# Bias seeds from ScalarE in a graph-network kernel: four layer-1 chunks of ten get their bias written into PSUM, and TensorE adds to it

## The chip, the cores and the metric

The kernel runs on one core of one Trainium2 chip. The metric is device time in microseconds (us), the median of three runs. The core has five engines with queues of their own: TensorE (PE in the profile, its weight loads PEld), VectorE (DVE), ScalarE (ACT), GpSimd (POOL) and SyncE (SP), whose queue issues most DMAs. Matmul results land in PSUM, eight banks of 512 float32 per partition. One instruction waits for another through semaphores, counters that an engine raises when an instruction ends.

## The reference

A message-passing layer over 128 graphs of 64 nodes with 128 channels. For each edge (i, j) a three-layer perceptron runs on the pair of node features; messages are masked by the adjacency matrix and summed over j; a second perceptron updates the node, with a residual.

```python
def _mlp(x, w0, b0, g0, be0, w1, b1, g1, be1, w2, b2):
    h = jax.nn.relu(x @ w0 + b0)
    h = _layernorm(h, g0, be0)
    h = jax.nn.relu(h @ w1 + b1)
    h = _layernorm(h, g1, be1)
    return h @ w2 + b2
pair_feats = jnp.concatenate([f_i, f_j], axis=-1)
messages = _mlp(pair_feats, msg_w0, ...) * coupling_matrix[..., None]
agg = jnp.sum(messages, axis=2)
upd_in = jnp.concatenate([part_feats, agg], axis=-1)
return part_feats + _mlp(upd_in, upd_w0, ...)
```

About one adjacency entry in seven is set, and the kernel computes only those.

## The kernel before

Edges are compacted: each of 64 pairs of graphs gets 2 x 640 slots, and slots are worked in chunks of 512 (four tiles of 128 edges). There are 160 chunks; five chunks are one quad of graphs `q`, ten one block `b` of eight graphs. The program is unrolled, and its order is written by hand: iteration `n` of the last loop runs layer 0 of chunk `n`, the statistics of chunk `n - 1`, and layer 1 of chunk `n - 8` (`L1 = 8`). Around these, `at(n, place, fn)` puts other work at fixed places of an iteration: "a" and "m" before layer 1, "b" between layer 1 and layer 0, "x" after the statistics, and so on. Each engine runs its own instructions strictly in the order in which the loop writes them. Two places matter most:

- **Layer 1** (`layer1`). The layer norms are folded: the layer-1 result of an edge is `relu(h @ w1c + std0 * b1b)`, where `std0` is the edge's standard deviation after layer 0, and `b1b` a bias row spread over 128 partitions. Before the change TensorE makes the term `std0 * b1b` itself. The root `m_sd` (ScalarE, `root0`) is split in a high and a low half `sh` (ScalarE, then GpSimd, L541 and L542), transposed by TensorE (L547, `turn_root`), copied to `sdT` (ScalarE, L552), and used as the weights of one 80x512 matmul against the table `b1t` (L561) that opens the PSUM bank `z`. Four pairs of `w1c` matmuls (L564) add the layer. ScalarE then writes `y` = relu(`z`) (L567). There is one `z` bank, so the next chunk's first matmul waits until `y` has read it; there is one `hps` bank for layer 0, emptied by ScalarE's `h` (L517).
- **The update unit** (`Unit`). Once a block, some twenty iterations later, a chain of steps runs for 512 nodes: `ysum`, transposes, a layer `uh`, its statistics, its root `um_sd`, `upd_shift` (ScalarE: four 128x128 copies `usdb` = `bu1b` times a column of `um_sd`, L724), a layer `uy` that adds `usdb`, and the output. `STEADY` lists the iterations of these steps for the first thirteen blocks.

In the steady part the work of an iteration depends on the last digit of its number. Iterations 4, 9 and 2 carry little besides the two layers; 8 and 3 carry 40 short matmuls of the message sums `ys` and 16 of the next rows `mu`; 5, 6, 7, 0 and 1 carry steps of the update. At iterations 1 and 6 the quad's root `m_sd` is taken. ScalarE also makes, per pair of graphs, `d` (L460) and the 32-bit copy `i` (L472), and per block `abh`, `xnT` and small copies.

The program's functions that the change touches:

Of the kernel before, what the change touches and what calls it, by code (L numbers as in the profile page):

```python
# [13 lines left out]
AF = mybir.ActivationFunctionType  # L14
# [9 lines left out]
def tile_gnn(  # L24
# [40 lines left out]
    nc = tc.nc  # L65
# [7 lines left out]
    QT = 4 * TG  # L73
    CH = 4
    QC = QT // CH
    NCHK = NQ * QC
    PB = 4
    NB = NP // PB
    CPB = NCHK // NB
# [88 lines left out]
    W = {}  # L168
# [83 lines left out]
    def root0(stp, m2, n, name):  # L252

        sd = stp.tile([P, n], F32, name=name + "_sd")
        nc.scalar.activation(sd, m2, AF.Sqrt, scale=1.0 / C, bias=eps_c)
        return sd
# [28 lines left out]
    def edge_path(es):  # L285
# [9 lines left out]
        stp = es.enter_context(tc.tile_pool(name="stp", bufs=5))  # L295
# [19 lines left out]
        def zbank():  # L315
            return ps_z.tile([P, CH, C], F32, name="z").rearrange("p t c -> p (t c)")
# [4 lines left out]
        def at(n, place, fn, *args):  # L321
            plan.setdefault((n, place), []).append((fn, args))
# [3 lines left out]
                fn(*args)  # L326

        blocks = {b: {} for b in range(NB)}
        TP, S, H, ST0, V0, SD, SH, Y, ST1, Q, OH, WT, YS, MK, D, IR, JR = ({} for _ in range(17))


        def load_adj(b):
# [196 lines left out]
        def eng_of(q):  # L529

            return nc.vector if q == NQ - 1 else nc.gpsimd
# [3 lines left out]

        def root_of(q):

            sd = root0(stp, V0[q], QT, "m20")
            SH[q] = lp.tile([P, 4, QT], F32R, name="sh", bufs=2)
            sdb = sd.unsqueeze(1).to_broadcast([P, 2, QT])  # L540
            nc.scalar.copy(SH[q][:, 0:2, :], sdb)  # L541
            eng_of(q).tensor_tensor(SH[q][:, 2:4, :], sdb, SH[q][:, 0:2, :].bitcast(F32),  # L542
                                    op=ALU.subtract)
# [6 lines left out]
        def root_out(q):  # L550
            t = lp.tile([4 * QT, P], F32R, name="sdT")
            nc.scalar.copy(t, SD[q][0:4 * QT, 0:P])  # L552
            SD[q] = t

        def layer1(n):

            q, c = divmod(n, QC)
            ps = (hbank if n >= NCHK - L1 and n % 2 else zbank)()
            ps = ps.rearrange("p (t c) -> p t c", t=CH)
            h = H.pop(n)  # L560
            nc.tensor.matmul(ps, lhsT=SD[q], rhs=W["b1t"][:, CH * c:CH * c + CH, :], start=True,  # L561
                             stop=False, skip_group_check=True)
            for t in range(CH):
                nc.tensor.matmul(ps[:, t, :], lhsT=h[:, t * P:(t + 1) * P], rhs=W["w1c"],  # L564
                                 start=False, stop=True, skip_group_check=True)
            Y[n] = yp.tile([P, CH, C], F32, name="y")
            nc.scalar.activation(Y[n], ps, AF.Relu)  # L567
# [92 lines left out]
        def wide(name, u):  # L660

            if name not in u.blk:
                u.blk[name] = updp.tile([P, PB, C], F32, name=name,
                                        bufs=2 if name in ("uo", "xo", "m0") else 1)
            return u.blk[name][:, u.q, :]
# [29 lines left out]
        def layer(u, *pairs):  # L695
            ps = u.bank()
            for q in range(u.n):
                s = slice(q * P, (q + 1) * P)
                for n, (src, w) in enumerate(pairs):
                    l = (u.blk["xnT"][:, (u.k0 + q) * P:(u.k0 + q + 1) * P] if src == "xn" else  # L700
                         getattr(u, src)[:, s])
                    nc.tensor.matmul(ps[:, s], lhsT=l, rhs=w, start=(n == 0),
                                     stop=(n == len(pairs) - 1))
            u.l_ps = ps[:, 0:u.n * P].rearrange("p (q c) -> p q c", q=u.n)
# [13 lines left out]
        def upd_root0(u):  # L718
            u.sd = root0(updp, u.m2, u.n, "um0" + u.tag)

        def upd_shift(u):
            u.usdb = wide("usdb", u)
            for q in range(u.n):
                nc.scalar.activation(u.usdb[:, q, :], W["bu1b"], AF.Copy, scale=u.sd[:, q:q + 1])  # L724

        def upd_m1(u):
# [21 lines left out]
        L1 = QC + 3  # L748
        SC = QC + L1 + QC

        STEADY = (1, 2, 3, 3, 4, 7, 8, 6, 8, 9, 12, 13, 11, 14, 15)
# [26 lines left out]
        for b in reversed(range(NB)):  # L778
            o = b * CPB
            n = o + QC + SC  # L780

            if b < NB - 1:
                t = STEADY if b < NB - 3 else LAST[b - NB + 3]
                units = [(Unit(b, 0, PB, nc.gpsimd, ubank), n, t, 0, t[5] - 1)]
                if b == NB - 2:
                    units = [units[0][:3] + (-5, -4)]
            else:
                units = [(Unit(b, 2, 2, nc.vector, zbank), NCHK + L1 + 1, LAST[3], 1, 1),
                         (Unit(b, 0, 2, nc.gpsimd, hbank), NCHK + L1 - 1, LAST[2], 3, 3)]
            for u, n, t, m0_at, xo_at in units:  # L790
                at(n + m0_at, "m", bias0, u)
                at(n + xo_at, "e", residual, u)
                at(n + t[0], "a", sums_out, u)
                at(n + t[1], "x", turn, u, "ysum")
                at(n + t[2], "a", turn_out, u, "ysum")
                at(n + t[3], "x", lambda u: layer(u, ("xn", u0a), ("ysumT", W["w2u"])), u)
                at(n + t[4], "m", layer_out, u, "uh", "m0")
                at(n + t[4], "e", upd_m0, u)
                at(n + t[5], "x", turn, u, "uh")
                at(n + t[6], "a", turn_out, u, "uh")  # L800
                at(n + t[7], "a", upd_root0, u)
                at(n + t[7], "x", upd_shift, u)
                at(n + t[8], "x", lambda u: layer(u, ("uhT", W["u1c"])), u)
                at(n + t[9], "m", layer_out, u, "uy", "usdb")
                at(n + t[9], "e", upd_m1, u)
                at(n + t[10], "x", turn, u, "uy")
                at(n + t[11], "a", turn_out, u, "uy")
                at(n + t[12], "a", upd_root1, u)
                at(n + t[12], "m", upd_inverse, u)
                at(n + t[13], "x", lambda u: layer(u, ("uyT", W["u2c"])), u)  # L810
                at(n + t[14], "m", finish, u)
        for p in range(NP):
            n = p * TG * 2 // CH
            if p > 1:
                at(max(n - 7, p - 2), "a", distance, p)
                at(max(n - 6, p - 2), "m", make_tp, p)
                at(max(n - 5, 1), "a", node_rows, p)
                at(max(n - 4, 1), "a", stack, p, 0, IR)
                for k in range(2):
                    at(n - 5 + k, "k", marks, p, k)  # L820
                    at(n - 5 + k, "k", compare, p, k)
                at(n - 3, "a", stack, p, 1, JR)
            w = p // 2 * QC + QC + L1 + p % 2
            last = p // 2 == NQ - 1
            at(w - 4, "a", node_marks, p)
            q, h = divmod(p, 2)
            for g in range(2):
                wait = h + 2 if q == NQ - 3 else h + 1 if q == NQ - 2 else 2 + (2 * h + g + 1) // 2
                at(*((NCHK + L1, "b") if last else (q * QC + QC + L1 + wait, "e1")), weights, p, g)
            at(NCHK + L1 + 1 if last else q * QC + SC - (q >= NQ - 3), "x1", reduce, p)  # L830
        for q in range(NQ):
            n = q * QC + QC
            last = q == NQ - 1
            at(n, "e0", var0_of, q)
            at(*((n, "e1") if last else (n + 1, "b")), root_of, q)
            at(*((n + 2, "b") if last else (n + 1, "x")), turn_root, q)
            at(n + 2, "x" if last else "a", root_out, q)
            at(n + L1 - last, "e1", var1_step, q)
            wait = 0 if last else 1 if q == NQ - 2 else 2
            at(n + L1 + wait, "a", root1_of, q)  # L840
            at(n + L1 + wait, "m", inverse_of, q)
# [26 lines left out]
        for g in range(2):  # L868
            s = slice(g * N, (g + 1) * N)
            nc.scalar.copy(S[0][0:N, g, :], TP[0][s])  # L870
            for k in range(2):
                c = slice(k * HC, (k + 1) * HC)
# [68 lines left out]
        for n in range(last + 1):  # L941
            run(n, "a")
            run(n, "m")
            if n == NCHK:
                stats0(n - 1)
            if 0 <= n - L1 < NCHK:
                layer1(n - L1)
            run(n, "b")
            if n < NCHK:
                layer0(n)  # L950
            if 0 <= n - 1 < NCHK - 1:
                stats0(n - 1)
            run(n, "k")
            if 0 <= n - L1 < NCHK:
                stats1(n - L1)
            for k in ("x", "x1", "x2", "e0", "e1", "e"):
                run(n, k)
# [3 lines left out]
    with ExitStack() as es:  # L961
        es.enter_context(tc.manual_schedule())
        flag = edge_path(es)
# [160 lines left out]
```

## Time and profile before

| what | value |
|---|---|
| median of three runs | 613.35 us (612.3 to 613.7) |
| profiled execution | 612.8 us, its span 611.1 us |
| TensorE busy | 574.7 us, 94% of the span |
| VectorE busy | 479.3 us, 78% |
| ScalarE busy | 397.2 us, 65% |
| GpSimd busy | 294.8 us, 48% |
| the `b1t` matmul, L561 into `z` | 156 times, mean 492 ns |
| layer-1 output `y`, L567 from `z` | 156 times, mean 597 ns |
| update copy `usdb`, L724 | 64 times, mean 396 ns |

The span is the stretch that the profiler sees; the time of the execution has 1.7 us more around it. In a row of the timeline the first number is the start in us from the start of the span, the second the length of the row in us, then engine, line, operation and `out<-in`; `x4` means four instructions merged into a row; square brackets give how long the engine was idle before the row and what released it. A mean length contains latency: instructions of one engine overlap at their ends, and what counts for the queue is the distance of starts.

### The profile page before, as it was taken

Reading aid. Unit: us, or ns where it says so; the run is one execution under the profiler, and the core shown is the slowest. Engines: PE = TensorE matmul, PEld = TensorE weight load, DVE = VectorE, ACT = ScalarE, POOL = GpSimd, SP = SyncE. Lnnn points to the kernel's source line nnn. Section 1 sums busy time; section 2 is a strip of 40 time slices with the busy share of each in tenths; the row PEclk is TensorE's granted clock in tenths of the full one; section 3 lists DMA queues with packets and bytes.
Section 4 is the critical chain, followed back from the end, with each engine's and each line's share of the span. In section 5 each row is a group of like instructions: output and inputs, shape, how many; then the busy total and the mean of one; then the engine's idle time right before and its main releaser. Section 6 shows DMA issues by size and latency. Waiting matters only on the chain. (4 is left out here: it accounts for less than half of the span.)

```text
span 611.1 us, 15571 instructions
## 1 busy us (share of the span) xinstructions
PE 574.7 (94%) x5393; PEld 530.1 (87%) x5393; DVE 479.3 (78%) x1947; ACT 397.2 (65%) x845; POOL 294.8 (48%) x837
## 2 busy tenths in 40 slices
PE   5798999999999999999999999999999999999895
PEld 4687889898989989898998989899898989989884
DVE  5767687886969788696978869697886969787675
ACT  5675666776666577666657766665776666566334
POOL 1632355644626564462656446265644626545352
PEclk7899999999999999999999999999999999999998
DMA  4554445455455655545453454545344354431201
GB/s 115 141 126 117 106 110 130 80 124 99 102 137 105 132 85 123 99 102 140 107 129 84 123 101 102 139 108 131 79 124 101 93 140 99 108 85 33 62 18 39
DMA packets 91087, 63.86 MB, mean 105 GB/s; under 512 B 57462, under 2 KB 74876, under 8 KB 91004
## 3 DMA queue, kind: packets, MB, share of 16 engines
q1 hardware_dynamic: 90716, 62.69, 44.7%
q8 instruction: 44, 0.72, 0.5%
q14 instruction: 39, 0.32, 0.2%
q10 hardware_dynamic: 288, 0.13, 0.1%
HBM read 6.82 MB, written 4.19 MB: 18 GB/s over the span
## 5 line engine op out<-in xcount | busy, mean ns | idle before, releaser
L527 DVE BATCH_NORM_STATS2 st<-hT 128x6 f32<-128x128 f32 x640 | 141.3, 283 | 63.0 <-PE hT L523 62.9
L564 PEld LDWEIGHTS z<-w1c,h 128*128 128x128 f32 x1248 | 164.1, 192 | 6.8
L564 PE MATMUL z<-w1c,h 128*128 128x128 f32 x1248 | 164.6, 275 | 0.0
L567 ACT ACTIVATE y<-z 128x512 f32<-128x512 f32 x156 | 93.1, 597 | 71.8 <-PE z L564 71.2
L574 DVE BATCH_NORM_STATS2 st<-y 128x6 f32<-128x128 f32 x640 | 137.6, 277 | 2.7 <-ACT y L567 1.4
L245 POOL TENSOR_TENSOR m_d<-st 128x20 f32<-128x20 f32 x62 | 17.1, 276 | 229.7 <-DVE st L527 206.3
L517 ACT ACTIVATE h<-hps,b0c 128x512 f32<-128x512 f32 x160 | 109.5, 684 | 2.5 <-PE hps L514 2.4
L523 PE MATMUL hT<-ident,h 128*128 128x128 f32 x640 | 97.2, 275 | 1.1 <-DVE st L527 1.1
L630 POOL TENSOR_TENSOR w<-oh,m_q 128x320 f32<-128x320 f16 x126 | 91.4, 742 | 10.1 <-PE hT L523 5.5
L514 PE MATMUL hps<-s,abl 128*128 128x512 f32 (+3 forms) x256 | 92.3, 373 | 0.4 <-ACT h L517 0.4
L561 PE MATMUL z<-b1t,sdT 80*128 80x512 f32 x156 | 76.7, 492 | 11.7 <-ACT y L567 11.7
L523 PEld LDWEIGHTS hT<-ident,h 128*128 128x128 f32 x640 | 76.3, 141 | 11.1 <-ACT h L517 1.3
L514 PE MATMUL hps<-s,abh 128*128 128x512 f32 (+3 forms) x256 | 78.5, 325 | 0.0
L444 ACT CAST abh<-mu 128x512 fp32r<-128x512 f32 x32 | 18.8, 586 | 91.1 <-PE mu L437 91.1
L643 PE MATMUL ys<-y,w 128*64 128x128 f32 x1280 | 76.9, 275 | 0.0
L643 PEld LDWEIGHTS ys<-y,w 128*64 128x64 f32 x1280 | 69.2, 137 | 7.0 <-issue 6.6
L496 DVE TENSOR_TENSOR j<-mk,cmpt 128x320 fp32r<-128x320 f32 x126 | 59.7, 474 | 1.6 <-PE mk L488 1.6
L460 ACT ACTIVATE d<-slot,mid 128x640 f16<-128x640 f16 x64 | 53.4, 834 | 0.0
L514 PEld LDWEIGHTS hps<-s,abl 128*128 128x128 f32 x256 | 49.5, 193 | 1.8 <-ACT i L472 0.9
L514 PEld LDWEIGHTS hps<-s,abh 128*128 128x128 f32 x256 | 49.6, 194 | 0.0
L561 PEld LDWEIGHTS z<-b1t,sdT 80*128 80x128 f32 x156 | 29.4, 189 | 21.9 <-ACT y L567 15.1
L472 ACT CAST i<-tp 128x640 fp32r<-128x640 f16 x63 | 45.3, 719 | 1.9 <-DVE tp L466 1.9
(215 smaller groups left out, 972.5 us busy)
## 6 DMA issues: line engine op xcount, KB each, us to landing
s<-i SPq DMA_DIRECT2D x126, 160.0 KB, 2.7
s<-j SPq DMA_DIRECT2D x126, 160.0 KB, 2.6
xn<-in_x_dram SPq DMA_DIRECT2D x15, 256.0 KB, 3.9
out_dram<-uo SPq DMA_DIRECT2D x15, 256.0 KB, 2.4
an<-in_adj_dram SPq DMA_DIRECT2D x16, 128.0 KB, 2.6
oh<-tp SPq DMA_TRANSPOSE x64, 2.7
xn<-in_x_dram SPq DMA_DIRECT2D x2, 128.0 KB
out_dram<-uo SPq DMA_DIRECT2D x2, 128.0 KB
```

Source lines behind the costliest of these rows:

```text
L460: nc.scalar.activation(D[p], slot, AF.Abs, bias=blocks[b]["mid"][:, q:q + 1], scale=-1.0)
L496: nc.vector.tensor_tensor(JR[p][:, c], MK.pop((p, k))[:, 0:HC], cmpt[:, c], op=ALU.is_equal)
L514: nc.tensor.matmul(ps[:, c:c + w], lhsT=ab[:, g % 4, :], rhs=s, start=(k == 0), stop=(k == 1))
L517: nc.scalar.activation(H[n], ps, AF.Relu, bias=b0c)
L523: nc.tensor.transpose(ps[:, t, :], H[n][:, t * P:(t + 1) * P], ident)
L527: nc.vector.bn_stats(ST0[q][:, CH * c + t, :], ps[:, t, :])
L561: nc.tensor.matmul(ps, lhsT=SD[q], rhs=W["b1t"][:, CH * c:CH * c + CH, :], start=True, stop=False, skip_group_check=True)
L564: nc.tensor.matmul(ps[:, t, :], lhsT=h[:, t * P:(t + 1) * P], rhs=W["w1c"], start=False, stop=True, skip_group_check=True)
L567: nc.scalar.activation(Y[n], ps, AF.Relu)
L574: nc.vector.bn_stats(ST1[q][:, CH * c + t, :], Y[n][:, t, :])
L630: (nc.vector if p == NP - 2 else nc.gpsimd).tensor_tensor(WT[p][:, :, g, :], OH[p][:, :, g * N:(g + 1) * N], Q[q][:, k:k + TG].unsqueeze(2 ...
L643: nc.tensor.matmul(YS[b][g * N:(g + 1) * N, k, :], lhsT=w[:, t, g, :], rhs=y, start=(t == 0), stop=(t == TG - 1))
```

## The change

For each chunk `n` from 1 to 150 whose last digit is 0, 1, 6 or 9, sixty chunks in all, ScalarE writes `std0 * b1b` into the `z` bank with four 128x128 activations ("seeds"), straight from the root `m_sd` and `b1b`. They are put at "b" of iteration `n + 7`, so behind the `y` that empties the bank and ahead of that iteration's `h`; by last digit they stand in iterations 7, 8, 3 and 6. In iteration 6 they stand ahead of the root `m_sd` too, which the plan puts behind them at the same place. One iteration later these chunks have no `b1t` matmul: the first `w1c` matmul adds to what is in the bank. The transposes and `sdT` stay, since the other chunks use them. Second, in blocks on the `STEADY` list the four `usdb` copies are no longer issued together: one in iteration 9, one in 0, two in 1.

```diff
+        def seed(n):
+            q, c = divmod(n, QC)
+            Z[n] = zbank().rearrange("p (t c) -> p t c", t=CH)
+            for t in range(CH):
+                k = CH * c + t
+                nc.scalar.activation(Z[n][:, t, :], W["b1b"], AF.Copy, scale=SR[q][:, k:k + 1])
...
         def layer1(n):
-            ps = (hbank if n >= NCHK - L1 and n % 2 else zbank)()
-            ps = ps.rearrange("p (t c) -> p t c", t=CH)
             h = H.pop(n)
-            nc.tensor.matmul(ps, lhsT=SD[q], rhs=W["b1t"][:, CH * c:CH * c + CH, :], start=True,
-                             stop=False, skip_group_check=True)
+            if n in Z:
+                ps = Z.pop(n)
+            else:
+                ps = (hbank if n >= NCHK - L1 and n % 2 else zbank)()
+                ps = ps.rearrange("p (t c) -> p t c", t=CH)
+                nc.tensor.matmul(ps, lhsT=SD[q], rhs=W["b1t"][:, CH * c:CH * c + CH, :],
+                                 start=True, stop=False, skip_group_check=True)
...
-        def upd_shift(u):
-            u.usdb = wide("usdb", u)
-            for q in range(u.n):
+        def upd_shift(u, q0, q1):
+            if q0 == 0:
+                u.usdb = wide("usdb", u)
+            for q in range(q0, q1):
                 nc.scalar.activation(u.usdb[:, q, :], W["bu1b"], AF.Copy, scale=u.sd[:, q:q + 1])
...
-                at(n + t[7], "x", upd_shift, u)
+                if t is STEADY:
+                    for k, q0, q1 in ((0, 0, 1), (1, 1, 2), (2, 2, PB)):
+                        at(n + t[7] + k, "x", upd_shift, u, q0, q1)
+                else:
+                    at(n + t[7], "x", upd_shift, u, 0, u.n)
...
+        for n in range(1, NCHK - L1 - 1):
+            if n % CPB in (0, 1, 6, 9):
+                at(n + L1 - 1, "b", seed, n)
```

The lines of the changed file lie some twelve further down from `layer1` on (`y` is L579 there, the `w1c` matmul L576, `usdb` L737). ScalarE's queue in iterations 6 and 7 of a steady block, before, with the counters that each instruction waits for (DMA counters are those of the DMA rings):

```order
L567 ACTIVATE y<-z 128x512 [waits PE_49]
L255 ACTIVATE m_sd<-m_4643,eps_c 128x20 [waits Pool_49]
L541 CAST sh<-m_sd 128x40 [waits Activation_49]
L517 ACTIVATE h<-hps,b0c 128x512 [waits PE_49]
L472 CAST i_4715<-tp 128x640 [waits DMAHW2_49,DMAHW1_49,DVE_49]
L552 CAST sdT<-ma 80x128 [waits PE_49]
L567 ACTIVATE y<-z 128x512 [waits PE_49]
L517 ACTIVATE h<-hps,b0c 128x512 [waits PE_49]
```

The same stretch in the changed kernel:

```order
L579 ACTIVATE y<-z 128x512 [waits PE_49]
L562 ACTIVATE z<-b1b,m_sd 128x128 [waits Activation_49] x4
L255 ACTIVATE m_sd<-m_4721,eps_c 128x20 [waits Pool_49]
L541 CAST sh<-m_sd 128x40 [waits Activation_49]
L517 ACTIVATE h<-hps,b0c 128x512 [waits PE_49]
L472 CAST i_4798<-tp 128x640 [waits DMAHW2_49,DMAHW1_49,DVE_49]
L552 CAST sdT<-ma 80x128 [waits PE_49]
L579 ACTIVATE y<-z 128x512 [waits PE_49]
L562 ACTIVATE z<-b1b,m_sd 128x128 [waits Activation_49] x4
L517 ACTIVATE h<-hps,b0c 128x512 [waits PE_49]
```

Four seeds stand behind each of the two `y`, and each of them waits for ScalarE's own counter; `m_sd`, `sh` and `h` moved behind them. ScalarE's queue from iteration 9 to the start of iteration 1, before:

```order
L517 ACTIVATE h<-hps,b0c 128x512 [waits PE_49]
L724 ACTIVATE usdb<-bu1b,um_sd 128x128 [waits Activation_49]
L724 ACTIVATE usdb<-bu1b,um_sd 128x128 x3
L472 CAST i_4290<-tp 128x640 [waits DMAHW2_49,DMAHW1_49,DVE_49]
L460 ACTIVATE d<-slot,mid 128x640
L269 ACTIVATE m_sq<-m_v,eps_c 128x20 [waits Pool_49]
L567 ACTIVATE y<-z 128x512 [waits PE_49]
L517 ACTIVATE h<-hps,b0c 128x512 [waits PE_49]
L693 COPY uhT<-ma 128x512 [waits PE_49]
```

And in the changed kernel:

```order
L517 ACTIVATE h<-hps,b0c 128x512 [waits PE_49]
L737 ACTIVATE usdb<-bu1b,um_sd 128x128 [waits Activation_49]
L472 CAST i_5001<-tp 128x640 [waits DMAHW1_49,DMAHW0_49,DVE_49]
L460 ACTIVATE d<-slot,mid 128x640
L269 ACTIVATE m_sq<-m_v,eps_c 128x20 [waits Pool_49]
L579 ACTIVATE y<-z 128x512 [waits PE_49]
L517 ACTIVATE h<-hps,b0c 128x512 [waits PE_49]
L737 ACTIVATE usdb<-bu1b,um_sd 128x128
L705 COPY uhT<-ma 128x512 [waits PE_49]
```

Three copies moved from ahead of `i` to behind the next `h` and into the iteration after it (not in these rows). TensorE's queue from the end of iteration 7 into iteration 8, before:

```order
L702 MATMUL mu<-u2c,uyT 128x128 [waits DVE_49]
L702 MATMUL mu<-u2c,uyT 128x128 x3
L561 MATMUL z<-b1t,sdT 128x512 [waits Activation_49]
L564 MATMUL z<-w1c,h 128x128 x4
L514 MATMUL hps<-s,abl 128x384 [waits Activation_49]
```

And in the changed kernel:

```order
L714 MATMUL mu<-u2c,uyT 128x128 [waits DVE_49]
L714 MATMUL mu<-u2c,uyT 128x128 x3
L576 MATMUL z<-w1c,h 128x128 [waits PE_49,Activation_49]
L576 MATMUL z<-w1c,h 128x128 x3
L514 MATMUL hps<-s,abl 128x384 [waits Activation_49]
```

The wait on ScalarE moved from the `b1t` matmul, where it stood for `y`, to the first `w1c` matmul, where it stands for the last seed; a wait on TensorE's own counter is added.

More of the change, by code (lines that the diff above doesn't have):

```diff
@@ L328, in edge_path @@
         blocks = {b: {} for b in range(NB)}
-        TP, S, H, ST0, V0, SD, SH, Y, ST1, Q, OH, WT, YS, MK, D, IR, JR = ({} for _ in range(17))
+        TP, S, H, ST0, V0, SD, SH, Y, ST1, Q, OH, WT, YS, MK, D, IR, JR, SR, Z = ({} for _ in range(19))
         def load_adj(b):
@@ L536, in root_of @@
         def root_of(q):
-            sd = root0(stp, V0[q], QT, "m20")
+            sd = SR[q] = root0(stp, V0[q], QT, "m20")
             SH[q] = lp.tile([P, 4, QT], F32R, name="sh", bufs=2)
```

## The prediction

> **What bounds the kernel now.** I read the page's totals first, then the costliest groups, then the waits, and last the timeline of one block of ten iterations, engine by engine. The totals:
>
> ```profile
> span 611.1 us, 15571 instructions
> PE 574.7 (94%) x5393; PEld 530.1 (87%) x5393; DVE 479.3 (78%) x1947; ACT 397.2 (65%) x845; POOL 294.8 (48%) x837
> ```
>
> TensorE (PE) is busy for 94% of the span, so the question is what holds its queue, and where it does not run. The groups (shapes kept apart) and the waits:
>
> ```profile
> L561 PE MATMUL z<-b1t,sdT 80*128 80x512 f32 x156 | 76.7, 492 | 11.7 <-ACT y L567 11.7
> L724 ACT ACTIVATE usdb<-bu1b,um_sd 128x128 f32<-128x128 f32 x64 | 20.4, 396 | 0.4 <-DVE uy L238 0.3
> ```
>
> ```profile
> PEld z L561 <- ACT y L567: 15.1, 14, 1.1
> PE z L561 <- ACT y L567: 11.7, 14, 0.9
> ```
>
> The first row is the matmul that four tenths of the chunks lose. The second is a ScalarE (ACT) copy of the very form that is added: 128x128, a table of the bias times a column, 396 ns each. The waits say that TensorE stands still at a known place: 14 times, 0.9 us (matmul) or 1.1 us (weight load) at the longest, a layer-1 group waits for ScalarE's `y`. I call an iteration by the last digit of its number: place 0 to place 9; there are sixteen blocks of ten. Here is ScalarE from place 9 to the end of place 0, then TensorE for the same stretch and for the start of places 3 to 5:
>
> ```profile
> 320.61 0.60 ACT L567 ACTIVATE y<-z 128x512 f32<-128x512 f32 x1 [0.53 <-PE z L564]
> 321.10 0.68 ACT L517 ACTIVATE h<-hps,b0c 128x512 f32<-128x512 f32 x1
> 321.67 1.27 ACT L724 ACTIVATE usdb<-bu1b,um_sd 128x128 f32<-128x128 f32 x4
> 322.84 0.72 ACT L472 CAST i<-tp 128x640 fp32r<-128x640 f16 x1
> ...
> 324.18 0.30 ACT L269 ACTIVATE m_sq<-m_v,eps_c 128x20 f32<-128x20 f32 x1
> 324.38 0.58 ACT L567 ACTIVATE y<-z 128x512 f32<-128x512 f32 x1
> ```
>
> ```profile
> 319.18 0.50 PE L561 MATMUL z<-b1t,sdT 80*128 80x512 f32 x1
> 319.51 1.05 PE L564 MATMUL z<-w1c,h 128*128 128x128 f32 x8
> ...
> 320.64 0.39 PE L514 MATMUL hps<-s,abh 128*128 128x512 f32 x1
> 320.87 0.60 PE L523 MATMUL hT<-ident,h 128*128 128x128 f32 x4
> 321.26 0.50 PE L561 MATMUL z<-b1t,sdT 80*128 80x512 f32 x1
> ...
> 323.53 0.60 PE L688 MATMUL ma<-ident,uh 128*128 128x128 f32 x4
> 325.02 0.51 PE L561 MATMUL z<-b1t,sdT 80*128 80x512 f32 x1 [0.89 <-ACT y L567]
> ...
> 330.47 0.50 PE L561 MATMUL z<-b1t,sdT 80*128 80x512 f32 x1
> ...
> 336.12 0.50 PE L561 MATMUL z<-b1t,sdT 80*128 80x512 f32 x1
> 336.46 1.05 PE L564 MATMUL z<-w1c,h 128*128 128x128 f32 x8
> ...
> 338.21 0.50 PE L561 MATMUL z<-b1t,sdT 80*128 80x512 f32 x1
> ```
>
> TensorE is done with place 0's transposes (323.53 plus about 0.43) near 323.96 and waits until 325.02. ScalarE is why: four `usdb` copies hold it from 321.67 to 322.84, so the row writer `i`, `d` and a root come late, and `y` starts only at 324.38 and ends at 324.96. Everywhere else in the block TensorE is the limit, with one tight spot at place 4, shown below.
>
> **What one removed matmul is worth.** From `b1t` to the first `w1c` matmul it takes 0.33 us at place 9 (319.18 to 319.51). The start before it moves up too, so the whole slot is not quite the saving: the four transposes ahead of `b1t` take 0.39 us (320.87 to 321.26), a little less than elsewhere. I take 0.30 us. From below the 0.23 us bounds it that another 512-column matmul holds the queue when transposes follow (320.64 to 320.87); from above 0.34, the slot at place 4 (336.12 to 336.46). The new first matmul also checks a second counter of its own engine, which may cost some hundredths; that is inside the bounds.
>
> The Trainium skill, "TensorE: Matmul & The Clock Gate", Part 1 ("Wait — 56ns, not 53.3ns?"), gives the start-to-start of a warm matmul as N/2.4 GHz plus 2.5 ns, 216 ns at N = 512; by it each removal saves only 0.216 us and the sum below is some 4 us smaller. The 0.33 us row stands above that rule, the 0.23 us row fits it.
>
> **What four seeds cost on ScalarE.** The rows for this and for the places that follow are those of place 6 and 7, all engines; look at ScalarE's `m_sd` and `sh` and at TensorE's L547, which needs them:
>
> ```profile
> 307.05 0.60 ACT L567 ACTIVATE y<-z 128x512 f32<-128x512 f32 x1 [0.39 <-PE z L564]
> 307.63 0.31 ACT L255 ACTIVATE m_sd<-m,eps_c 128x20 f32<-128x20 f32 x1
> 307.97 0.22 ACT L541 CAST sh<-m_sd 128x40 fp32r<-128x40 f32 x1
> 308.39 0.27 POOL L542 TENSOR_TENSOR sh<-m_sd,sh 128x40 fp32r<-128x40 f32 x1
> ...
> 309.68 0.12 PEld L547 LDWEIGHTS ma<-ident,sh 128*80 128x80 f32 x1
> ...
> 310.13 1.05 PE L564 MATMUL z<-w1c,h 128*128 128x128 f32 x8
> 311.22 0.60 ACT L567 ACTIVATE y<-z 128x512 f32<-128x512 f32 x1 [0.86 <-PE z L564]
> ...
> 313.35 0.84 ACT L460 ACTIVATE d<-slot,mid 128x640 f16<-128x640 f16 x1
> 313.55 0.48 PE L561 MATMUL z<-b1t,sdT 80*128 80x512 f32 x1
> ```
>
> Each block has 16 of them, 240 in all, about 0.4 us each. Each one waits on ScalarE's own counter: the first for the `y` that empties the bank, the others for the seed before. So they cannot overlap as `usdb` does (four in 1.27 us by the timeline, a start every 0.29 us). One link costs its full 396 ns and a hand-over. The hand-over I take from `m_sd` to `sh`, in these rows: 307.63 plus 0.31, then 307.97, 0.03 us. From the start of `y` to the end of the last seed: 0.60 + 0.03 + 4 x 0.396 + 3 x 0.03 = 2.30 us, and TensorE sees it 0.05 us later, as it sees `y` (320.61 plus 0.60, and `b1t` at 321.26). No row shows ScalarE writing to PSUM. Bounds for one seed: 0.22 us (`sh`, fewer columns) and 0.60 us (`y`, four times the columns); I take 0.396, the row with the same shape and operands.
>
> The Trainium skill, "ScalarE: Activation LUTs", The pipeline for one element, says that a write to PSUM has the lower latency, with no figure; by it the chain would be shorter and the gain larger.
>
> **Place 6, where it hurts.** The seeds stand between `y` (307.05) and `m_sd`. `y` ends at 307.65; seeds start at 307.68, 308.11, 308.53, 308.96, and the last ends at 309.36. `m_sd` can start 0.29 behind the last seed's start, 309.25, `sh` at 309.59, done 309.81. Behind it on its queue wait the next `h`, `i` and `sdT`, all in time for place 7's later uses; on POOL three `w` products wait behind its half of `sh`, and they are not read before place 8's sums. But POOL's `sh` moves from 308.39 to about 309.89, ends at 310.16, and L547, the transpose at the end of place 6, moves from 309.68 to 310.21. That is a new wait of 0.53 us on TensorE, right in front of the seeded group that saves 0.30.
>
> **Place 7 and 8.** Place 7's group moves from 310.13 to 310.13 + 0.53 - 0.30 = 310.36, its `y` from 311.22 to 311.45, its seeds end at 313.75. TensorE asks for them at 313.55 + 0.53 - 0.30 = 313.78: just in time, and 0.30 saved. ScalarE is then late: with the slots of `h` (0.57), `xnT` and two small copies (0.64), `d` starts near 314.85 instead of 313.35, and the `y` of place 8 near 315.58. Its seeds end near 317.88, and place 9 asks for them only near 319.18 + 0.53 - 0.60 = 319.11: place 8 is 5.63 us long and swallows it. Another 0.30. The same holds at place 3, 5.65 us long (330.47 to 336.12).
>
> **Place 9 and 0.** Without `b1t`, `y` moves from 320.61 to 320.31 and `h` to 320.80. One copy instead of four: 321.37 to 321.66. `i`, `d` and the root then take 1.54 us as before (322.84 to 324.38), so `y` starts at 323.20, ends at 323.78, and place 1's `b1t` starts at 323.83 instead of 325.02. That is 1.19 us, 0.30 of it from the matmul and 0.89 from the spread copies. TensorE's own work would allow 323.66, so 0.17 us of waiting is left. The copies moved to place 0 and 1 lie beside TensorE: ScalarE is free about 0.2 us before the `y` of places 1 and 2.
>
> **Place 4.** Here ScalarE is the limit between 336.12 and 338.21:
>
> ```profile
> 336.24 0.59 ACT L444 CAST abh<-mu 128x512 fp32r<-128x512 f32 x1 [3.12 <-PE mu L437]
> 336.72 0.59 ACT L669 COPY ysum<-ys 128x512 f32<-128x512 f32 x1
> 337.20 0.31 ACT L269 ACTIVATE um_sq<-um_v,eps_c 128x4 f32<-128x4 f32 x1
> 337.55 0.60 ACT L567 ACTIVATE y<-z 128x512 f32<-128x512 f32 x1
> ```
>
> `abh`, `ysum` and the small root follow the row matmuls of place 3, which do not move against this start. The root before `y` takes a slot of 0.20 us at place 0 (324.18 to 324.38); here too, 337.20 plus 0.20, so `y` can start at 337.40, not 337.25: 0.15 us saved, not 0.30.
>
> **The two ends.** Early blocks have no update work to cover the chain. At place 6 and 7 of the second block:
>
> ```profile
> 61.11 0.60 ACT L567 ACTIVATE y<-z 128x512 f32<-128x512 f32 x1 [1.70 <-PE z L564]
> ```
>
> ```profile
> 62.63 0.31 PE L547 MATMUL ma<-ident,sh 128*80 128x128 f32 x1 [0.41 <-POOL sh L542]
> 63.82 0.50 PE L561 MATMUL z<-b1t,sdT 80*128 80x512 f32 x1
> 66.68 0.48 PE L561 MATMUL z<-b1t,sdT 80*128 80x512 f32 x1
> ```
>
> `y` at 61.11 gives last seed 63.41, `sh` on POOL until 64.22, L547 at 64.27: a wait of 1.65 us. Place 7 is 2.86 us long, 2.56 without `b1t`; the chain needs 1.43 - 0.30 + 2.30 + 0.05 = 3.48, a wait of 0.92. Place 7 of the third and of the last block is as short.
>
> **The sum.** A regular block: 0.15 (place 4) - 0.53 (6) + 0.30 (7) + 0.30 (8) + 1.19 (9 and 0) = 1.41 us. Blocks three to thirteen, counted from 0, are regular: 11 x 1.41 = 15.5. Block 2: 0.30 - 0.53 + 0.30 - 0.92 + 0.30 + 1.19 = 0.64. Block 14, with a shorter place 7: about 1.1. The tail in block 15: -0.65. Blocks 0 and 1: -1.65 - 0.92 and four savings of 0.30, -1.4 (the ends are estimates at the same prices; of their rows only the dearest stand above). Together 15.3 us. The profiled execution took 612.8 us (span 611.1), which gives 597.5; the median of the runs is 0.55 us above that execution, which gives 598.
>
> **Rivals.** First, the chain is quick: seeds overlap or a write to PSUM is short, so that four end before `sh` is missed. The wait at place 6 goes (15 times 0.53) and part of the short ones: about 9 us more, 589 us. For it: `usdb` at one start every 0.29 us. Against it: each seed's own wait.
>
> Second, the matmul's slot is worth less, or a new wait eats the spread copies' share. At 0.23 us, the 46 savings counted in full lose 0.07 each, 3.2 us: 601, still in my forecast's own range, and 0.15 of its chance is for that. If VectorE, busy 78% of the span, or POOL's variances are late at place 0, the 13 x 0.89 go instead and about 4 us are left: 610. Against it: VectorE itself waits there, for TensorE and for the root.
>
> Third, on the other side: a seed into PSUM is dearer than a copy into SBUF. The chain ends in a TensorE wait at place 6 and again at place 7, 30 places of four links, so each further 0.1 us a seed costs 12 us. Break-even lies at 0.396 + 15.3/120 = 0.52 us a seed; at the 0.60 of `y` the time is 613.35 - 15.3 + 24.5 = 623. For it: no row shows the form. Against: `y` carries four times the elements.
>
> **Chances.** My forecast, 593 to 605 us: 0.58. The quick chain: 0.12. The small gain, 605 to 612: 0.15. Slower: 0.12. No change within 0.2% (about what a measurement here can tell): 0.03. So faster 0.85, same 0.03, slower 0.12. The range runs from 589, the quick chain, to 610, the second rival's far end, and leaves out the slower case and little else.
>
> **What the profile afterwards should show.** `b1t` matmuls drop from 160 to 100. 240 seeds near 0.40 us that start about 0.43 us apart. The wait of `z` for `y` at place 0 falls from 0.9 to about 0.2 us each. New: TensorE's L547 waits for POOL's `sh` about 0.5 us in most blocks, more in the second. At place 7 next to no wait for a seed, at 8 and 3 none. I am wrong if seeds start 0.3 us apart or take over 0.5, if L547 does not wait, or if places 7 to 9 do not shorten by 0.2 to 0.34 us each.

## The result and the profile after

The changed kernel takes 598.41 us (median of 4, 597.76 to 599.39) against 613.03 for the kernel before in the same set: ratio 0.9763, 95% interval 0.9744 to 0.9782. The prediction was 598 us. The profiled execution took 597.76 us with a span of 596.1. The page's totals:

```profile
span 596.1 us, 15749 instructions
PE 564.7 (95%) x5333; PEld 518.7 (87%) x5333; DVE 479.4 (80%) x1947; ACT 480.4 (81%) x1085; POOL 294.8 (49%) x837
```

ScalarE went from 397.2 to 480.4 us of busy time, TensorE from 574.7 to 564.7. The groups that changed, with shapes kept apart:

```profile
L562 ACT ACTIVATE z<-b1b,m_sd 128x128 f32<-128x128 f32 x240 | 89.2, 372 | 7.8
L573 PE MATMUL z<-b1t,sdT 80*128 80x512 f32 x96 | 47.1, 491 | 0.6 <-ACT y L579 0.2
L737 ACT ACTIVATE usdb<-bu1b,um_sd 128x128 f32<-128x128 f32 x64 | 23.3, 397 | 0.4 <-DVE uy L238 0.3
```

240 seeds at 372 ns, a little shorter than the `usdb` copies at 397 ns; 96 `b1t` matmuls into `z` are left of 156. The waits that answer to those of before (total in us, times, longest); first a line of before that belongs beside them:

```profile
PEld ma L547 <- POOL sh L542: 4.9, 4, 2.3
```

and then those of the changed kernel:

```profile
PEld ma L547 <- POOL sh L542: 12.2, 18, 2.3
PEld z L573 <- ACT y L579: 4.0, 14, 0.5
PEld z L576 <- ACT z L562: 2.7, 4, 0.8
PE ma L547 <- POOL sh L542: 8.3, 18, 2.0
PE z L576 <- ACT z L562: 2.0, 4, 0.7
```

A layer-1 group still waits for `y` 14 times, now 4.0 us in all at the weight load instead of 15.1. In its place L547 waits for POOL's `sh` 18 times, 12.2 us, where it was 4 times and 4.9 us, and four groups wait for a seed. ScalarE and GpSimd at place 6:

```profile
301.10 0.60 ACT L579 ACTIVATE y<-z 128x512 f32<-128x512 f32 x1 [0.38 <-PE z L576]
301.74 1.58 ACT L562 ACTIVATE z<-b1b,m_sd 128x128 f32<-128x128 f32 x4
303.25 0.30 ACT L255 ACTIVATE m_sd<-m,eps_c 128x20 f32<-128x20 f32 x1
303.58 0.22 ACT L541 CAST sh<-m_sd 128x40 fp32r<-128x40 f32 x1
...
303.88 0.27 POOL L542 TENSOR_TENSOR sh<-m_sd,sh 128x40 fp32r<-128x40 f32 x1 [1.41 <-ACT sh L541]
...
304.20 0.12 PEld L547 LDWEIGHTS ma<-ident,sh 128*80 128x80 f32 x1 [0.40 <-POOL sh L542]
...
304.35 1.06 PE L576 MATMUL z<-w1c,h 128*128 128x128 f32 x8
```

The four seeds start 0.04 us after `y` ends (301.70) and take 1.58 us, so they start (1.58 - 0.372) / 3 = 0.403 us apart: 372 ns and a hand-over of 0.03. `m_sd`, `sh` and GpSimd's part follow in a row, GpSimd idle for 1.41 us ahead of it, and L547 starts its load at 304.20 after 0.40 us of waiting. Places 9 to 1, ScalarE and then TensorE:

```profile
315.41 0.40 ACT L737 ACTIVATE usdb<-bu1b,um_sd 128x128 f32<-128x128 f32 x1
315.71 0.72 ACT L472 CAST i<-tp 128x640 fp32r<-128x640 f16 x1
...
317.25 0.59 ACT L579 ACTIVATE y<-z 128x512 f32<-128x512 f32 x1
```

```profile
313.15 1.16 PE L576 MATMUL z<-w1c,h 128*128 128x128 f32 x8
314.07 0.47 PE L514 MATMUL hps<-s,abl 128*128 128x512 f32 x1
...
315.00 0.49 PE L573 MATMUL z<-b1t,sdT 80*128 80x512 f32 x1
...
317.26 0.60 PE L700 MATMUL ma<-ident,uh 128*128 128x128 f32 x4
317.90 0.50 PE L573 MATMUL z<-b1t,sdT 80*128 80x512 f32 x1
```

With one copy ahead of `i`, `y` starts at 317.25 and place 1's `b1t` at 317.90, 4.75 us behind the start of place 9 at 313.15; before it was 5.84 (319.18 to 325.02), there counted from a `b1t`.

In the steady part every block repeats to 0.02 us. The distance from one layer-1 group's first matmul to the next, read from TensorE's timeline for one block of each kernel (iterations 70 to 79), in us:

| place | before | spread only | seeds only | changed | root first | no bias |
|---|---|---|---|---|---|---|
| 0 | 3.76 | 2.89 | 3.76 | 2.89 | 2.89 | 2.89 |
| 4 | 2.08 | 2.08 | 1.93 | 1.93 | 1.93 | 1.92 |
| 6 | 4.17 | 4.17 | 4.66 | 4.66 | 4.26 | 4.25 |
| 7 | 3.73 | 3.72 | 3.49 | 3.49 | 3.49 | 3.50 |
| 8 | 5.63 | 5.63 | 5.32 | 5.31 | 5.32 | 5.31 |
| 9 | 2.08 | 2.08 | 1.85 | 1.84 | 1.85 | 1.85 |
| block | 35.63 | 34.74 | 35.15 | 34.28 | 33.89 | 33.89 |

Places 1, 2, 3 and 5 are equal in all six to 0.02 us. The last four columns are experiments told below. One reading caution: a group counts from the row of its first matmul, `w1c` or `b1t`, so a saving can appear one place away from its matmul. Place 6 in the kernel with no bias is 0.08 longer than before, with no wait at all.

The stretch ahead of the first layer-1 group differs between the profiled executions too: it ends between 32.6 and 34.5 us, and the edits do not touch it. So where two kernels lie close, I also give the time from the start of the first layer-1 group to the start of the last, read from the traces: 551.05 us before, 536.41 changed.

### The profile page after: what moved, and what is told of

The parts are those of the page before. It is cut to its first block, busy times and chain, and to the rows that moved or that the text cites. A ratio compares the mean times of both kernels' runs of the same rounds, so it can differ in the third digit from the quotient of the medians.

```text
span 596.1 us, 15749 instructions
## 1 busy us (share of the span) xinstructions
PE 564.7 (95%) x5333; PEld 518.7 (87%) x5333; DVE 479.4 (80%) x1947; ACT 480.4 (81%) x1085; POOL 294.8 (49%) x837
## 4 chain that ended last, share of the span: by engine, by line
## 5 line engine op out<-in xcount | busy, mean ns | idle before, releaser
L576 PE MATMUL z<-w1c,h 128*128 128x128 f32 x1248 | 168.2, 278 | 2.0 <-ACT z L562 2.0
L576 PEld LDWEIGHTS z<-w1c,h 128*128 128x128 f32 x1248 | 159.6, 192 | 11.9 <-issue 5.0
L579 ACT ACTIVATE y<-z 128x512 f32<-128x512 f32 x156 | 93.5, 599 | 36.5 <-PE z L576 33.3
L562 ACT ACTIVATE z<-b1b,m_sd 128x128 f32<-128x128 f32 x240 | 89.2, 372 | 7.8
L573 PE MATMUL z<-b1t,sdT 80*128 80x512 f32 x96 | 47.1, 491 | 0.6 <-ACT y L579 0.2
```

The lines of the kernel that those rows point to most:

```text
L562: nc.scalar.activation(Z[n][:, t, :], W["b1b"], AF.Copy, scale=SR[q][:, k:k + 1])
```

## The experiments

**The spread copies alone.** `e1_spread_only` keeps all `b1t` matmuls and has no seeds:

```diff
-        for n in range(1, NCHK - L1 - 1):
-            if n % CPB in (0, 1, 6, 9):
-                at(n + L1 - 1, "b", seed, n)
```

> Only the spread of the update copies, no seeds: all 160 b1t matmuls stay. My theory: it ends the 0.89 us wait at place 0 in 13 blocks and nothing else, 13 x 0.89 = 11.6 us, so 601.4 us. Rival, that the seeds carry the gain and the spread copies come back as waits at places 1 and 2: 608 us or more.

Measured: 601.27 us, ratio 0.9812 (0.9794 to 0.9831) to 613.15. Only place 0 changed. The wait for `y` falls as in the changed kernel, from 15.1 us to 3.7:

```profile
PEld z L573 <- ACT y L579: 3.7, 14, 0.5
```

So most of the gain, 11.9 of about 14.6 us, comes from the smaller half of the change.

**The seeds alone.** `e2_seeds_only` issues the four update copies together again:

```diff
-                if t is STEADY:
-                    for k, q0, q1 in ((0, 0, 1), (1, 1, 2), (2, 2, PB)):
-                        at(n + t[7] + k, "x", upd_shift, u, q0, q1)
-                else:
-                    at(n + t[7], "x", upd_shift, u, 0, u.n)
+                at(n + t[7], "x", upd_shift, u, 0, u.n)
```

> Only the seeds, the four update copies together as before. My theory: the seeds net 15.3 - 11.6 = 3.7 us, since the new wait at place 6 and the short places give back most of what the lost matmuls save: 609.3 us. Rival, that the 60 lost matmuls are worth their full slot (60 x 0.30 = 18 us): 595 us.

Measured: 609.62 us, ratio 0.9957 (0.9939 to 0.9975): 3.5 us by the medians, 1.5 to 3.7 by the interval, from sixty lost matmuls and 240 added copies. From the first layer-1 group to the last it is 2.8 us.

```profile
PEld z L573 <- ACT y L579: 15.1, 14, 1.1
PEld ma L547 <- POOL sh L542: 12.1, 18, 2.3
```

Both waits stand side by side here: the old one for `y`, untouched, and the new one of L547. The two halves add up: 11.9 + 3.5 = 15.4 against 14.6 measured together, within the intervals (11.5 + 2.8 against 14.6 from the first layer-1 group to the last).

**What the matmuls are worth.** `e4_no_bias` has the spread copies, no seeds, and this edit:

```diff
-                nc.tensor.matmul(ps, lhsT=SD[q], rhs=W["b1t"][:, CH * c:CH * c + CH, :],
-                                 start=True, stop=False, skip_group_check=True)
+                bare = 1 <= n < NCHK - L1 - 1 and n % CPB in (0, 1, 6, 9)
+                if not bare:
+                    nc.tensor.matmul(ps, lhsT=SD[q], rhs=W["b1t"][:, CH * c:CH * c + CH, :],
+                                     start=True, stop=False, skip_group_check=True)
...
-                                 start=False, stop=True, skip_group_check=True)
+                                 start=bare, stop=True, skip_group_check=True)
```

> As the changed kernel without the seeds: the sixty chunks get no std0 times bias at all, neither from TensorE nor from ScalarE, so this shows what the lost matmul is worth when nothing takes its place. My theory, 0.30 us at places 7, 8 and 9 (45 times) and 0.15 at place 4: 16 us below the kernel with the spread copies alone, 585.5 us; so the seeds themselves cost about 13 us in the changed kernel. Rival, a matmul is worth 0.216 us: 589.5 us.

Measured: 587.58 us, ratio 0.9592 (0.957 to 0.9615). That lies between my figure and the rival's, and the steady block decides: against the spread alone it is 0.85 us shorter, 0.16 of it at place 4, so the other three matmuls are worth 0.69 / 3 = 0.23 us each, the lower bound of the prediction and near the rival's 0.216. TensorE at the places 6 to 9 of this kernel:

```profile
263.93 0.27 PE L547 MATMUL ma<-ident,sh 128*80 128x128 f32 x1
264.04 1.06 PE L578 MATMUL z<-w1c,h 128*128 128x128 f32 x8
...
267.54 1.06 PE L578 MATMUL z<-w1c,h 128*128 128x128 f32 x8
...
272.85 1.16 PE L578 MATMUL z<-w1c,h 128*128 128x128 f32 x8
```

From L547's matmul to the first `w1c` matmul it takes 0.11 us here. The same stretch before:

```profile
309.56 0.39 PE L702 MATMUL mu<-w2u,ysumT 128*128 128x128 f32 x2
309.79 0.27 PE L547 MATMUL ma<-ident,sh 128*80 128x128 f32 x1
309.81 0.48 PE L561 MATMUL z<-b1t,sdT 80*128 80x512 f32 x1
310.13 1.05 PE L564 MATMUL z<-w1c,h 128*128 128x128 f32 x8
```

L547 to `b1t` took 0.02 us and `b1t` to `w1c` 0.32, 0.34 together, so leaving `b1t` out shortens this stretch by 0.23. The 0.02 us is the trap: the two `mu` matmuls ahead take 0.23 us together, 0.11 each, and L547 takes 0.11 as well once `w1c` follows it. So the row of `b1t` starts some 0.09 us inside L547's time, and the slot read from that row holds time of the matmul ahead. Counted from the start of the matmul ahead, less that one's own 0.11, the trace of before gives 0.34 - 0.11 = 0.23. At place 9 the 0.11 us shows inside the group: with `b1t` the next matmul followed the first `w1c` by 0.81 us (319.51 to 320.32 before), without it by 0.92 (313.15 to 314.07 in the changed kernel). So 0.1 us of the 0.33 us slot was not the matmul's: it comes back as soon as another matmul stands first. What inside TensorE causes it these runs do not show.

The seeds' own price is the difference to the changed kernel: 598.41 - 587.58 = 10.8 us by the medians, 9.8 from the first layer-1 group to the last (536.41 against 526.66).

**The root ahead of the seeds.** `e3_root_first` registers the seeds after the roots, so that at place 6 `m_sd` and `sh` come first:

```diff
-        for n in range(1, NCHK - L1 - 1):
-            if n % CPB in (0, 1, 6, 9):
-                at(n + L1 - 1, "b", seed, n)
         for p in range(NP):
...
             at(n + L1 + wait, "m", inverse_of, q)
+        for n in range(1, NCHK - L1 - 1):
+            if n % CPB in (0, 1, 6, 9):
+                at(n + L1 - 1, "b", seed, n)
```

> As the changed kernel, but at place 6 the root m_sd and its split sh stand ahead of the four seeds on ScalarE, not behind them. My theory: L547 no longer waits there (0.49 us in 13 blocks, about 1.6 us in the second block), the seeds end at 4.1 us after the start of place 6, just before place 7 asks for them at 4.15, so about 8 us are gained: 590 us. Rival: the same four links now end too late for place 7 and TensorE waits there instead, 597 to 599 us.

Measured: 593.01 us, ratio 0.9676 (0.9646 to 0.9707), 5.4 us faster than the changed kernel.

```profile
265.99 0.60 ACT L579 ACTIVATE y<-z 128x512 f32<-128x512 f32 x1 [0.38 <-PE z L576]
266.56 0.31 ACT L255 ACTIVATE m_sd<-m,eps_c 128x20 f32<-128x20 f32 x1
266.91 0.22 ACT L541 CAST sh<-m_sd 128x40 fp32r<-128x40 f32 x1
267.04 1.58 ACT L562 ACTIVATE z<-b1b,m_sd 128x128 f32<-128x128 f32 x4
268.55 0.67 ACT L517 ACTIVATE h<-hps,b0c 128x512 f32<-128x512 f32 x1
```

```profile
PEld ma L547 <- POOL sh L542: 4.9, 4, 2.3
PEld z L576 <- ACT z L562: 3.0, 5, 0.8
```

L547's waits are back at 4.9 us in 4 places, what they were before the change, and the seeds still end in time: the block is 33.89 us, the same as with no bias at all. There the seeds cost nothing. I missed by 3 us because the wait was worth 0.40 us a block and not 0.49 (0.08 of that was the later row from which the next group counts), and because in the second block it only moved: iteration 16 is 5.62 us long here and 5.76 in the changed kernel. L547 waits there no longer than before, but `beb`, a small ScalarE copy of the start-up, now stands behind the seeds, and TensorE waits for it:

```profile
65.14 0.49 PE L203 MATMUL mu<-u,beb 128*128 128x128 f32 x2 [1.55 <-ACT beb L202]
```

In the third block nothing was gained either: iterations 26 and 27 take 4.66 and 3.36 us in the changed kernel, 4.52 and 3.49 here, with a wait for the seeds themselves.

**A longer chain.** `e5_five_links` writes the first tile's seed twice:

```diff
                 nc.scalar.activation(Z[n][:, t, :], W["b1b"], AF.Copy, scale=SR[q][:, k:k + 1])
+                if t == 0:
+                    nc.scalar.activation(Z[n][:, t, :], W["b1b"], AF.Copy, scale=SR[q][:, k:k + 1])
```

> As the changed kernel with a fifth link in each chain: the first of the four seeds is written twice, 0.40 us more per chain. My theory, that each chain ends in a TensorE wait at place 6 and, past a slack of about 0.14 us, at place 7, and nowhere else: 15 x 0.40 + 12 x 0.26 + 3 x 0.40 = 10.3 us, 608.7 us. Rival one, the prediction's slope without the slack: 30 x 0.40 = 12 us, 610.5 us. Rival two, ScalarE as a whole has become the bound: all 60 chains cost 0.40 us, 24 us, 622 us.

Measured: 609.25 us, ratio 0.9957 (0.9938 to 0.9976), for 60 x 0.40 = 24 us of ScalarE work. Against the changed kernel that is 10.8 us by the medians, 11.9 by the two ratios, and 12.7 from the first layer-1 group to the last (549.11).

```profile
PEld ma L547 <- POOL sh L542: 18.2, 18, 2.7
PEld z L578 <- ACT z L562: 7.1, 16, 1.2
```

L547's wait grew from 12.2 to 18.2 us, and waits for a seed from 4 to 16: the chains of places 6 and 7, as said. In the steady block place 6 grew by 0.40 us, place 7 by 0.27 and place 8 by 0.11, since the group that waits for its seed at the start of place 8 also takes 0.92 us instead of 0.81 to pass. So the chain of place 7 costs 0.38 of its 0.40 us: the slack of 0.14 us that I counted on was not there. The medians cannot tell 608.7 from 610.5, but the steady block (0.79 us longer) and the traces speak for the first rival, without the slack. Places 3 and 8 still hide their chains, which rules out the second rival: ScalarE is not the bound as a whole; two of four chains a block are exposed.

**A shorter chain.** `e6_one_link` fills the bank with one 128x512 activation:

```diff
-            for t in range(CH):
-                k = CH * c + t
-                nc.scalar.activation(Z[n][:, t, :], W["b1b"], AF.Copy, scale=SR[q][:, k:k + 1])
+            k = CH * c
+            nc.scalar.activation(Z[n], W["b1b"].unsqueeze(1).to_broadcast([P, CH, C]), AF.Copy,
+                                 scale=SR[q][:, k:k + 1])
```

> As the changed kernel, but one 128x512 activation writes the whole bank, scaled by the standard deviations of the chunk's first tile alone, so the bias of the other three tiles is wrong; the chain is about 1.33 us long instead of 2.26. My theory: the wait of L547 at place 6 goes (0.41 us in 13 blocks) and most of the waits at the short places 16, 17, 27 and 157, about 9 us together, 589.5 us, and nothing is gained beyond the kernel without any bias (587.6). Rival: the length of the chain does not matter and the wait at place 6 has another cause, 597 to 599 us.

Measured: 590.49 us, ratio 0.9639 (0.9622 to 0.9657).

```profile
L561 ACT ACTIVATE z<-b1b,m_sd 128x512 f32<-128x512 f32 x60 | 41.5, 692 | 1.9
```

One link of 692 ns in place of four: L547's extra wait is gone in the steady part (0.7 us of it is left in iteration 16), and so is the wait at place 7 of the short blocks. The length of the chain is the cause, and the first rival's 589 us was a fair price for a quick one.

**Three chunks of ten.** `e7_three_of_ten` drops the chunks that end in 9:

```diff
-            if n % CPB in (0, 1, 6, 9):
+            if n % CPB in (0, 1, 6):
```

> As the changed kernel with seeds for three chunks of ten, without those that end in 9 (written at place 6). My theory: each such chunk costs 0.41 us of L547's wait and saves 0.23 us of a matmul, so leaving them out gains 0.18 us in 12 blocks, some 1.5 us in the second block and 0.2 in the last: about 594.5 us. Rival: the fourth seeded chunk still pays, 600 us or more.

Measured: 595.24 us, ratio 0.9704 (0.9677 to 0.9731). Faster than the change with less of it, and L547's wait is what it was before: a matmul of 0.23 us is not worth a wait of 0.40. Its interval lies wholly below that of the changed kernel.

```profile
PEld ma L547 <- POOL sh L542: 4.8, 4, 2.3
```

**The best version.** `e8_root_first_long_places` takes the root first and keeps the matmul for the five chunks whose chain falls in a short iteration:

```diff
-            if n % CPB in (0, 1, 6, 9):
+            if n % CPB in (0, 1, 6, 9) and n not in (1, 9, 10, 20, 150):
```

> Root first at place 6, and the chunks 1, 9, 10, 20 and 150, whose chains are written in iterations too short to hide them, keep their b1t matmul. My theory: the waits for seeds at iterations 16, 17 and 27 go, 1.9 + 0.45 us, and 0.1 at the end, against the kernel with the root first: 590.6 us. Rival: these waits are hidden work of the start-up and nothing changes, 593 us.

Measured: 589.88 us, ratio 0.9629 (0.96 to 0.9658): faster than both kernels. Against the root first alone it is 3.1 us, but the two come from different sets (593.01 and 589.88, with 613.15 and 612.38 before them) and their intervals overlap, so its share is not settled by the times. From the first layer-1 group to the last the traces differ by 2.6 us (530.75 and 528.14), nearly all of it in the blocks of the five chunks. They show the mechanism too: iterations 16 and 17, 5.62 and 3.46 us there, are 4.12 and 2.85 here. At iteration 16 this ends the wait for `beb` told above, not one for seeds as I expected. Of the loads' waits for a seed 0.4 us is left, in the last column of this group (shapes kept apart):

```profile
L576 PEld LDWEIGHTS z<-w1c,h 128*128 128x128 f32 x1248 | 159.6, 191 | 9.8 <-issue 5.0 <-ACT z L562 0.4
```

## Why the prediction was right, point by point

- **Where the time was.** Right: the wait at place 0 (0.89 us predicted, 0.87 measured) was the largest term, and the copies moved to places 0 and 1 cost nothing there. The rest of waiting that I left at place 0, 0.17 us, is 0.21 by the same count (four transposes from 317.26 take 0.43 us, and `b1t` starts at 317.90).
- **The chain at place 6.** Right in mechanism, the new wait of L547 for POOL's `sh`; too dear. The wait cost 0.40 us a block, not 0.53, for two reasons. I took 396 ns from `usdb` for a form that no row showed; into PSUM it is 372 ns, and since `m_sd` starts 0.30 us behind the last seed's start, three start-to-start links count, 0.403 instead of 0.426 us, 0.07 in all. The rest is a reading: I followed L547's weight load, which before ran 0.11 us ahead of its matmul (309.68 and 309.79). From the start of `y` the load moved from 2.63 to 3.10 us, the matmul only from 2.74 to 3.11 (304.21 in the changed kernel). The Trainium skill, "ScalarE: Activation LUTs", The pipeline for one element, says that PSUM is the lower-latency destination; these runs agree, with 372 against 397 ns.
- **The matmul's worth.** Mis-sized: 0.30 us in the sum, 0.23 measured. The step that failed is the reading of the slot from `b1t` to `w1c` as the saving: it held 0.1 us that stays when the matmul goes. The second counter that the first `w1c` checks shows no cost: at place 8 it starts as late behind the last `mu` matmul in the changed kernel as in the kernel with no bias, 0.11 us. The Trainium skill, "TensorE: Matmul & The Clock Gate", Part 1 ("Wait — 56ns, not 53.3ns?"), would have given 0.216, and I set its rule below the 0.33 us row; the measured 0.23 stands close to the rule.
- **The two errors cancelled.** A block: 0.16 - 0.40 + 3 x 0.23 + 0.87 = 1.32 from the terms, 1.35 in the trace, 1.41 predicted. That the total came so close is luck in part: with the wait right and the matmul wrong I would have been some 2 us too low, the other way round 3 us too high, both inside the range.
- **Place 4.** Right: 0.15 predicted, 0.15 to 0.16 measured, also with no seeds at all, so the limit there is ScalarE's row of copies and not the chain. In iteration 24, where the small root ahead of `y` is missing, the place gives the full 0.23 (2.08 to 1.85).
- **Place 7 in a regular block.** Right, just in time; the fifth link showed that there was next to no slack, 0.38 us lost of 0.40.
- **The ends.** Right in sign. Iteration 16 went from 4.12 to 5.76 us (1.65 us of wait predicted at L547, which moved from 2.93 to 4.51 us behind the start), iteration 17 from 2.86 to 3.47 (3.48 predicted). Counted by the prediction's blocks, from place 1 to the next place 1, the traces give -1.56 us for block 1 and nothing for block 0 (-1.4 predicted for both), 0.54 for block 2 (0.64), 1.34 for each regular block (1.41), 1.13 for block 14 (1.1) and -0.21 for the tail (-0.65).
- **The rivals.** The quick chain and the slower case both turn on the length of the chain, and both prices held where they were tried: one link gives 590.5 (589 said), and 0.40 us more per chain cost 10.8 us by the medians and 12.7 by the traces, where the break-even was worked out with 12 us. VectorE or POOL coming late at place 0, the far end of the second rival, did not happen: that place gave its 0.87 us.

## What to carry to other kernels

When work moves from a full engine to one with idle time, ask at each place what stands behind it in the receiving engine's queue: here four copies were free at three places of four in a regular block and cost 0.40 us at the fourth, because a small root waited behind them. The slot from an instruction's own start to the next start can hold time of its neighbours; count from the start of the instruction ahead and take off that one's own slot, or leave the instruction out once and measure, before paying for a replacement. And look first for waits of the full engine that a mere change of order ends, since that was four fifths of the gain.

## What the runs showed of the hardware that I had not expected

A 128x128 ScalarE activation with a per-partition scale took 372 ns into PSUM and 397 ns into SBUF in the same kernel. Four that each wait for the one before start 0.403 us apart, where `usdb` copies without such waits start 0.29 us apart; one 128x512 activation did the same area in 692 ns. And a `b1t` matmul whose slot to the next start read 0.32 to 0.34 us was worth 0.23 wherever it was left out and TensorE was the limit: behind L547 the rest was time of the matmul ahead, and at place 9 the `w1c` group took 0.11 us longer to pass without it (0.92 against 0.81 us).
